# Cross-attention block: block 29 projected in seven products of halves, block 31's query products 1 and 7 in quarters, banks and order written anew

## The chip, the cores and the metric

One core of one Trainium2 chip. The time is that of the device for one launch, in microseconds. PE is TensorE, DVE VectorE, ACT ScalarE, POOL GpSimd; SP issues most transfers.

## The reference

A cross-attention block with adaptive layer norm, in float32. x is 16 x 1024 x 512, the context 16 x 64 x 512, 16 heads of 32.

```python
def _ada_ln(x, c, W_ss, b_ss):
    mu = jnp.mean(x, axis=-1, keepdims=True)
    var = jnp.mean((x - mu) ** 2, axis=-1, keepdims=True)
    h = (x - mu) / jnp.sqrt(var + EPS)
    ss = jax.nn.silu(c) @ W_ss + b_ss
    scale, bias = jnp.split(ss, 2, axis=-1)
    return (1.0 + scale)[:, None, :] * h + bias[:, None, :]
xq = _ada_ln(x_q, t_vec, Wss_q, bss_q)
xkv = _ada_ln(x_kv, t_vec, Wss_kv, bss_kv)
q = (xq @ Wq + bq).reshape(B, Lq, nh, dh)
kv = (xkv @ Wkv + bkv).reshape(B, Lkv, 2, nh, dh)
k, v = kv[:, :, 0], kv[:, :, 1]
scores = jnp.einsum('bqhd,bkhd->bhqk', q, k) / jnp.sqrt(jnp.float32(dh))
attn = jax.nn.softmax(scores, axis=-1)
out = jnp.einsum('bhqk,bkhd->bqhd', attn, v).reshape(B, Lq, H)
return x_q + (out @ Wp + bp)
```

## The kernel before

The queries are worked in 32 blocks of 512 rows (two per batch entry), numbered 0 to 31. The context is worked once, in two groups A and B of eight entries, on the way in.

Large products are not done plainly. A query projection of a block (512 x 512 by 512 x 512) is split into halves and done as seven products of halves instead of eight, by the scheme of Strassen and Winograd: `query_product(i, 1..7)`, each four matmuls of 128x256 (each matmul is two passes on PE, so eight records in the profile). For blocks 4 to 30 the products 1 and 7 are split once more, into seven products of 128x128 each (`quarter_products`, four first and three later, with `quarter_copies` on ACT, three small adds `quarter_adds` on DVE between them, and `feature_quarters` on POOL ahead). The output projection is done in the same manner: `product(i, 1..7)`, with row sums of `ot` on POOL (`row_sum`), sums of weights WT, and results added to the residual r on DVE (`added`, L1116, and L1107 for block 31). Before, block 29 was the one exception: `project`, L974, four plain products, each of four matmuls of 128x512.

The steps of one block, in the order in which its data passes them:

- load x, statistics (`q_stats`, DVE), normalise (`hidden`, ACT), 32x32 transposes to ht (`turn`, DVE), sixteen DMAs to xt (`move`, SP), scale and shift (`scale_features`, ACT), sums of features (`feature_sums`, POOL);
- query products, copied to qt with bias (`query_out`, ACT, L645) or added to it (`query_added`, DVE);
- scores in two halves of the keys, z = 0 and 1 (`score_products`, L738), in two PSUM pairs of banks, `ps`; their maxima per row (`maximum`, DVE, L755) and copies to SBUF (`copied`, ACT);
- `maxima`: both halves' maxima joined and spread to a tile mb (DVE, L784); `subtract`: s minus mb (POOL, L797, one for each half); `weights`: the exponential (ACT, L808);
- `total`: the sum of both halves (POOL, L858); `row_total`: its row sums lt (DVE, L863); `inverse_rows`: the reciprocal (DVE, L878), a DMA to DRAM (ltd) and four back (vr); `spread_rows`: spread to vb (DVE, L891);
- `mix`: weights times values into the pairs po (PE, L936; L947 for blocks 30 and 31); `divided`: po times vb to ot (DVE, L915);
- the output projection, its results added to r, r written out.

Four blocks are in flight. The order on every engine is the order in which these functions are called: on the way in and on the way out a list written out by hand or by a planner, in the middle a `for` loop (i = 3 to 29) that calls each step for the block it is due for. Engines run their instructions in that order and wait for each other by semaphores only. `scores(i)` of a round works beside the query products of block i + 1 and the output products of blocks i - 2 and i - 1.

Of the kernel before, what the change touches and what calls it, by code (L numbers as in the profile page):

```python
# [15 lines left out]
P = 128  # L16
# [4 lines left out]
def cross_attention_block(  # L21
# [182 lines left out]
    BW = 32  # L204
# [526 lines left out]
    def score_products(i, z):  # L731
# [13 lines left out]
        if z == 0:  # L745
            m_tiles[i] = small.tile([P, 2, HPC, NJ], F32, tag="m2", name=f"m2_{i}")
# [51 lines left out]

    l_tiles = {}
# [14 lines left out]

    def again(i, g):
# [7 lines left out]
    def sums(i, z):  # L823
        if z == 0:
            l_tiles[i] = small.tile([P, 2, HPC, NJ], F32, tag="l2", name=f"l2_{i}", bufs=1)
# [35 lines left out]
    def row_total(i):  # L861
        lt_tiles[i] = small.tile([P, HPC, NJ], F32, tag="lt", name=f"lt_{i}", bufs=2)
# [8 lines left out]
    def halves_total(i):  # L871
        lt_tiles[i] = small.tile([P, HPC, NJ], F32, tag="lt", name=f"lt_{i}", bufs=2)
        both(lt_tiles[i].rearrange("p r j -> p (r j)"), l_tiles.pop(i), ALU.add)

    def inverse_rows(i):
# [3 lines left out]
        v = small.tile([P, NC, NJ], F32, tag="vr", name=f"vr_{i}", bufs=2)  # L879
# [4 lines left out]
        vt_rows[i] = v  # L884

# [133 lines left out]
    def biased(i, k):  # L1019

        b = b_first if k == 2 else b_diff
        if i == NB - 1 and k == 2:
            z_halves.append(bank(f"pp_{i}_0", 0))
            z_halves.append(ps_s.tile([P, 2, TB], F32, tag="s", name=f"pp_{i}_0b")[:, 0, :])
# [10 lines left out]
    def output_seed(i):  # L1035

        seeded.add((i, 2))
        acc[3] = bank(f"pp_{i}_2", 3)
        nc.scalar.copy(acc[3], acc[2])
# [24 lines left out]
    def product(i, n):  # L1064
# [12 lines left out]
        if n == 2 and (i, 2) not in seeded:  # L1077
            acc[k] = bank(f"pp_{i}_{n}", k)
        for t in range(2):
            for c in range(HC):  # L1080
# [12 lines left out]
                )  # L1093

# [29 lines left out]
    w_k_sums = big.tile([P, 4, HC, HO], F32, tag="big2", name="w_k_sums")  # L1124
    warm = bank("warm", 1)
    for _ in range(WARM):
        nc.tensor.transpose(warm[:, :P], ident, ident)
    load_x("A")
    load_scale_shift("kv", w_ss_kv, 0)
    q_stats("A", (0,))  # L1130
    q_stats("A", (1,))
    q_stats("A", (2,))
    load_scale_shift("kv", w_ss_kv, 1)
    q_stats("A", (3,))
    q_scale("A")
    load_context_weights(1, 0)
    hidden("A", (0,))
    biases()
    load_context_weights(0, 1)
    scale_shift_rows("kv", 0)  # L1140
    scale_shift_taken("kv", 0)
    turned_features("A", 0)
    hidden("A", (2,))
    hidden("A", (1,))
    turned_features("A", 1)
    hidden("A", (3,))
    scale_shift("kv", 2 * NC, 0)
    turned_features("A", 2)
    turned_features("A", 3)
    modulated("A", 0, 1, nc.vector)  # L1150
    load_context_weights(0, 0)
    modulated("A", 0, 0, nc.scalar)
    scale_shift_rows("kv", 1)
    scale_shift_taken("kv", 1)
    load_x(0)
    modulated("A", 0, 0, nc.vector)
    modulated("A", 0, 1, nc.scalar)
    load_scale_shift("q", w_ss_q, 0)
    column_sums("k", w_k_sb, w_k_sums, (0,))
    scale_shift("kv", 2 * NC, 1)  # L1160
    load_scale_shift("q", w_ss_q, 1)
    column_sums("k", w_k_sb, w_k_sums, (1,))
    modulated("A", 1, 0, nc.scalar)
    column_sums("k", w_k_sb, w_k_sums, (2,))
    modulated("A", 1, 0, nc.vector)
    context_product("A", "v", 1)
    context_product("A", "k", 2)
    modulated("A", 1, 1, nc.vector)
    load_x("B")
    modulated("A", 1, 1, nc.scalar)  # L1170
    feature_sums("A", nc.vector, (0,))
# [697 lines left out]
```

## Time and profile before

| | |
|---|---|
| three runs | 996.85, 997.28, 998.1 us; median 997.28 |
| span of the profiled execution | 996.9 us (the page gives no other time of it) |
| PE busy | 984.2 us |
| DVE, POOL busy | 895.6, 895.4 us |
| ACT busy | 779.3 us |
| granted TensorE clock | 1.000 mean |

Rows of a timeline read: start in us from the span's start, length, engine, line, operation, output<-inputs, shape, count; in brackets the idle time of that engine ahead of the row and what ended it. Matmuls are pipelined, so of PE the distance from one start to the next counts, not the length. In the chain of waits a row is start, length and what ran.

### The profile page before, as it was taken

What the parts mean: (1) busy time and instruction counts of PE and PEld (TensorE: products, weight loads), DVE (VectorE), ACT (ScalarE), POOL (GpSimd) and SP (SyncE); (2) the same over time, 40 slices, a digit from 0 to 9 for tenths busy, and PEclk for the clock granted to TensorE, in tenths of its full rate; (3) what the DMA queues carried; (4) which work ended last, traced back from release to release, by engine and by line L of the source; (5) the groups of instructions that cost most, each with busy time, mean ns of one, the idle gap of its engine ahead of it and who ended that gap; (6) DMA issues with size and microseconds to landing.
All of it is one profiled execution on the core that took longest, in us unless ns stands there. A gap on an engine that the chain in (4) does not pass through costs nothing.

```text
span 996.9 us, 20564 instructions
## 1 busy us (share of the span) xinstructions
PE 984.2 (99%) x7465; PEld 760.7 (76%) x7465; DVE 895.6 (90%) x1318; ACT 779.3 (78%) x1165; POOL 895.4 (90%) x690
## 2 busy tenths in 40 slices
PE   7999999999999999999999999999999999999998
PEld 6878777787777877877778778777787787777756
DVE  7696899999999999999999999999999999987786
ACT  3878878888888888888888888888888888876620
POOL 2677899999999999999999999999999999999681
PEclk9999999999999999999999999999999999999999
DMA  9765655555655555566655555665555555544422
GB/s 308 264 165 151 156 164 156 140 165 180 190 181 176 159 165 152 151 182 186 183 176 152 173 145 155 185 188 178 176 150 175 151 154 182 148 132 130 145 85 97
DMA packets 115188, 165.77 MB, mean 166 GB/s; under 512 B 34920, under 2 KB 46464, under 8 KB 113168
## 3 DMA queue, kind: packets, MB, share of 16 engines
q1 hardware_dynamic: 114704, 163.93, 55.2%
q8 instruction: 59, 0.97, 0.4%
q0 software_dynamic: 384, 0.54, 0.2%
q14 instruction: 41, 0.34, 0.1%
HBM read 79.47 MB, written 34.60 MB: 114 GB/s over the span
## 4 chain that ended last, share of the span: by engine, by line
PE 88%; DMA 4%; DVE 3%; SPq 2%; POOL 1%; issue 1%; ACT 0%; DVEq 0%; POOLq 0%
PE pp L1086 36%; PE pq L534 27%; PE pq L605 10%; PE ps L738 6%; PE po L936 5%; PE pk_A L534 1%; PE pk_B L534 1%; DMA w_k_sb<-in_L_xcond_Wkv_dram 1%; DMA r<-in_x_dram 1%; PE pv_B L534 1%; DMA ltd<-lt 1%; DMA V_B<-stage_B 1%; DMA vr<-ltd 0%; POOL sum L858 0%; DVE l L826 0%
## 5 line engine op out<-in xcount | busy, mean ns | idle before, releaser
L797 POOL TENSOR_TENSOR s<-s,mb 128x2048 f32<-128x2048 f32 x64 | 290.6, 4564 | 20.3 <-DVE mb L784 13.4
L1086 PE MATMUL pp<-w_p_sb,ot 128*128 128x256 f32 x740 | 174.8, 379 | 1.1 <-DVE ot L915 1.1
L764 ACT COPY s<-ps 128x1024 f32<-128x1024 f32 x128 | 129.3, 1013 | 46.1 <-PE ps L738 34.0
L755 DVE TRANSPOSE_TENSOR_REDUCE m<-ps 128x32 f32<-128x1024 f32 x128 | 152.4, 1228 | 10.4 <-PE ps L738 9.3
L1086 PEld LDWEIGHTS pp<-w_p_sb,ot 128*128 128x128 f32 x740 | 138.2, 190 | 20.5 <-issue 2.8
L645 ACT ACTIVATE qt<-pq,bias_t 128x256 f32<-128x256 f32 x256 | 107.8, 475 | 48.8 <-PE pq L605 27.7
L858 POOL TENSOR_TENSOR sum<-s,p 128x2048 f32<-128x2048 f32 x30 | 136.5, 4549 | 1.6 <-ACT p L808 1.6
L1116 DVE TENSOR_TENSOR r<-pp,r 128x512 f32<-128x512 f32 x183 | 120.3, 669 | 13.8 <-ACT xt L442 6.8
L534 PE MATMUL pq<-xt,w_q_sums 128*128 128x256 f32 x512 | 123.8, 385 | 0.0
L534 PEld LDWEIGHTS pq<-xt,w_q_sums 128*128 128x128 f32 x512 | 95.0, 190 | 34.6 <-issue 22.6
L1086 PE MATMUL pp<-WT,ot 128*128 128x256 f32 x492 | 118.4, 383 | 0.0
L1086 PE MATMUL pp<-WT,s 128*128 128x256 f32 x488 | 116.1, 380 | 1.3 <-DVE r L1107 0.8
L817 ACT ACTIVATE s<-s 32x2048 f32<-32x2048 f32 x60 | 114.6, 1910 | 1.8 <-DMA p<-s 0.4
L1086 PEld LDWEIGHTS pp<-WT,ot 128*128 128x128 f32 x492 | 90.9, 190 | 19.1 <-issue 4.2
L1086 PEld LDWEIGHTS pp<-WT,s 128*128 128x128 f32 x488 | 88.2, 190 | 13.1 <-POOL s L1056 1.3
L327 ACT ACTIVATE x<-x,rstdq 128x512 f32<-128x512 f32 x128 | 94.8, 807 | 1.0 <-POOL rstdq L304 1.0
L442 ACT ACTIVATE xt<-xt,ss_q 128x512 f32<-128x512 f32 x124 | 94.0, 809 | 1.0 <-DMA xt<-ht 0.7
L915 DVE TENSOR_TENSOR ot<-po,vb 128x1024 f32<-128x1024 f32 x62 | 73.0, 1219 | 17.6 <-PE po L936 17.4
L286 DVE BATCH_NORM_STATS2 bs<-x 128x6 f32<-128x512 f32 x128 | 85.3, 666 | 0.0
L493 POOL TENSOR_TENSOR xt_sums<-xt 128x512 f32<-128x512 f32 x64 | 81.2, 1269 | 2.0 <-DMA x<-in_x_dram 1.3
L357 DVE STREAM_TRANSPOSE ht<-x 128x512 f32<-128x512 f32 x124 | 77.7, 679 | 4.7 <-DMA xt<-ht 2.2
L891 DVE STREAM_TRANSPOSE vb<-vr 128x2048 f32<-128x2048 f32 (+1 forms) x33 | 73.7, 2236 | 4.4 <-DMA vr<-ltd 4.4
(224 smaller groups left out, 1963.8 us busy)
## 6 DMA issues: line engine op xcount, KB each, us to landing
x<-in_x_dram SPq DMA_DIRECT2D x32, 1024.0 KB, 5.3
r<-in_x_dram SPq DMA_DIRECT2D x32, 1024.0 KB, 5.9
xt<-ht SPq DMA_DIRECT2D x488, 64.0 KB, 2.0
out_dram<-r SPq DMA_DIRECT2D x60, 512.0 KB, 4.7
p<-s SPq DMA_DIRECT2D x60, 256.0 KB, 3.8
wss_kv<-in_L_xcond_Wss_kv_dram SPq DMA_DIRECT2D x4, 512.0 KB, 7.2
wss_q<-in_L_xcond_Wss_q_dram SPq DMA_DIRECT2D x4, 512.0 KB, 11.0
vr<-ltd SPq DMA_DIRECT2D x128, 8.0 KB, 1.7
```

Source lines behind the costliest of these rows:

```text
L327: nc.scalar.activation(dst, src, AF.Identity, bias=rstd[:, 1, j : j + 1], scale=rstd[:, 0, j : j + 1])
L442: nc.scalar.activation(xt[:, :, c, :], xt[:, :, c, :], AF.Identity, scale=ss["q"][:, c, b : b + 1], bias=ss["q"][:, NC + c, b : b + 1],)
L534: nc.tensor.matmul(out_, lhsT=lhsT, rhs=rhs, start=new and m == 0 and c == 0, stop=c == HC - 1, skip_group_check=True,)
L605: nc.tensor.matmul(qa["q", k][:, q * P : (q + 1) * P], lhsT=lhsT, rhs=rhs, start=first and q == 0, stop=True, skip_group_check=True,)
L645: nc.scalar.activation(dst, src, AF.Identity, bias=bq_t[:, o : o + 1])
L755: nc.vector.tensor_reduce(m_tiles[i][:, z, 2 * e : 2 * e + 2, :], s_banks[i, z][e].rearrange("p r (j a) -> p r j a", a=32), AX.X, ALU.max, ...
L764: nc.scalar.copy(s_tiles[i, z][:, 2 * e : 2 * e + 2, :], s_banks[i, z][e])
L797: eng.tensor_tensor(s_tiles[i, z], s_tiles[i, z], mb_tiles[i], ALU.subtract)
L817: nc.scalar.activation(s_tiles[i, 0][at + 32 : at + 64], raw_tiles[i][at : at + 32], AF.Exp, scale=SCALE)
L858: nc.gpsimd.tensor_tensor(t, s_tiles[i, 0], s_tiles[i, 1], ALU.add)
L1086: nc.tensor.matmul(to, lhsT=rows[:, c, t * P : (t + 1) * P], rhs=cols[:, c, :], start=n == 2 and (i, 2) not in seeded and t == 0 and c == ...
L1116: nc.vector.tensor_add(r, a, r)
```

## The change

Four things.

Block 29 is projected by `product(29, 1..7)` like its neighbours, with the bias seeded in PSUM (`biased`, `output_seed`) instead of added to r on POOL; `load_projection(again=True)`, which restored a part of w_p that the weight sums overwrite, is not called any more. Block 30's product 1 is no longer added by itself but seeds the bank of its product 2, as in the blocks before.

Block 31's query products 1 and 7 are done in quarters, 14 matmuls of 128x128 instead of 8 of 128x256.

For block 30, `subtract` of half 1 is done by DVE straight from PSUM (`lowered`), and its copy on ACT goes. Banks and buffers are laid anew (`acc_bank`; lt and vr with one buffer instead of two). A number of new functions is defined and not called (`inner_...`, `exchanged`, `reciprocal_rows` and others); two small constant tiles of theirs are made.

The order is new everywhere. The `for` loop now runs over i = 5 to 27 and is cut at another place: a round begins with the query products of block i and ends with its scores; the blocks before and after are written out. On the way in, the two halves of w_k are loaded in the other order, and product 1 of group A's keys runs ahead of product 2.

```diff
-    load_context_weights(0, 1)
...
-    load_context_weights(0, 0)
+    load_context_weights(0, 0)
+    load_context_weights(0, 1)
...
-        if n == 2 and i >= NB - 2:
-            return 1 if i == NB - 2 else 3
-        return (2 if n in (1, 6, 5, 3) else 3) - (2 if i == NB - 1 else 0)
+        if i == NB - 1 and n == 2:
+            return 4
+        return (2 if n in (1, 6, 5, 3) else 3) - (2 if i in (NB - 3, NB - 1) else 0)
...
+    def lowered(i, e):
+        rs = slice(2 * e, 2 * e + 2)
+        nc.vector.tensor_tensor(
+            s_tiles[i, 1][:, rs, :], s_banks[i, 1][e], mb_tiles[i][:, rs, :], ALU.subtract
+        )
...
-        lt_tiles[i] = small.tile([P, HPC, NJ], F32, tag="lt", name=f"lt_{i}", bufs=2)
+        lt_tiles[i] = small.tile([P, HPC, NJ], F32, tag="lt", name=f"lt_{i}", bufs=1)
...
-    for i in range(3, NB - 2):
+    for i in range(5, NB - 4):
...
+            row_total(a)
...
+        added(b, 7)
+        score_products(i, 0)
+        maximum(i, 0, 0)
...
-    project(y - 1, 0)
+    product(y - 1, 1)
```

In the steady blocks, DVE, from the row sums lt of block 20 to the joined maxima of block 21. A name is tile, block, part, and a running number: `r_19<-pp_19_3` is the add of a product of block 19's output projection (bank 3 holds products 7, and 4), `ps_21_0_1` the second pair of the scores of block 21's half 0. Before:

```order
L863 TENSOR_REDUCE lt_20_6399<-sum_20_6342 128x64
L878 RECIPROCAL lt_20_6399<-lt_20_6399 128x64
L755 TENSOR_REDUCE m2_21_6440<-ps_21_0_0_6422 128x32
L755 TENSOR_REDUCE m2_21_6440<-ps_21_0_1_6423 128x32
L622 TENSOR_TENSOR t_quarters_129<-pq_22_1_6443,t_quarters_129 128x128
L623 TENSOR_TENSOR pq_22_1_6443<-pq_22_1_6443,t_quarters_129 128x256
L624 TENSOR_TENSOR pq_22_1_6443<-pq_22_1_6443,t_quarters_129 128x128
L1116 TENSOR_TENSOR r_19_6143<-pp_19_2_6317,r_19_6143 128x2x256
L755 TENSOR_REDUCE m2_21_6440<-ps_21_1_1_6457 128x32
L755 TENSOR_REDUCE m2_21_6440<-ps_21_1_0_6456 128x32
L775 TENSOR_REDUCE m_21_6496<-m2_21_6440 128x64
L784 STREAM_TRANSPOSE mb_21_6498<-m_21_6496 128x2048
```

And now (L907 is the old L863, L1288 the old L1116, L922 the old L878):

```order
L907 TENSOR_REDUCE lt_20_6380<-sum_20_6335 128x64
L1288 TENSOR_TENSOR r_19_6071<-pp_19_3_6367,r_19_6071 128x2x256
L772 TENSOR_REDUCE m2_21_6419<-ps_21_0_0_6401 128x32
L772 TENSOR_REDUCE m2_21_6419<-ps_21_0_1_6402 128x32
L639 TENSOR_TENSOR t_quarters_129<-pq_22_1_6423,t_quarters_129 128x128
L640 TENSOR_TENSOR pq_22_1_6423<-pq_22_1_6423,t_quarters_129 128x256
L641 TENSOR_TENSOR pq_22_1_6423<-pq_22_1_6423,t_quarters_129 128x128
L1288 TENSOR_TENSOR r_19_6071<-pp_19_2_6312,r_19_6071 128x2x256
L922 RECIPROCAL lt_20_6380<-lt_20_6380 128x64
L772 TENSOR_REDUCE m2_21_6419<-ps_21_1_1_6446 128x32
L772 TENSOR_REDUCE m2_21_6419<-ps_21_1_0_6445 128x32
L792 TENSOR_REDUCE m_21_6499<-m2_21_6419 128x64
```

The add of product 7 (bank 3), which came after mb, stands behind lt, and the reciprocal has moved from there to behind the other add.

On the way out, PE around the first scores of block 31 (`pq_31` are its query products, `pp_28` the output products of block 28, `po_29` the mix of block 29). Before:

```order
L534 MATMUL pq_31_7_8846<-xt_sums_517,w_q_sb_101 128x256 x4
L534 MATMUL pq_31_1_8799<-xt_31_8501,w_q_sums_401 128x256 x4
L1086 MATMUL pp_28_2_8706<-WT_1338,s1_28_8703 128x256 x4
L738 MATMUL ps_31_0_0_8884<-qt_31_8843,K_B_131 32x512 x2
L738 MATMUL ps_31_0_1_8885<-qt_31_8843,K_B_131 32x512 x2
```

And now:

```order
L1002 MATMUL po_29_1_8909<-p_29_8723,V_B_133 32x512
L551 MATMUL pq_31_7_8857<-xt_sums_529,w_q_sb_101 128x256 x4
L551 MATMUL pq_31_1_8764<-xt_31_8532,w_q_sums_404 128x256 x4
L755 MATMUL ps_31_0_0_8943<-qt_31_8851,K_B_131 32x512 x2
L755 MATMUL ps_31_0_1_8944<-qt_31_8851,K_B_131 32x512 x2
```

The output product that stood between the last query product and the scores is gone from there.

Later on PE, the end of block 29's projection and block 30's. Before (128x512 are block 29's plain products):

```order
L974 MATMUL pp_29_2_9051<-w_p_sb_104,ot_29_8949 128x512 x4
L974 MATMUL pp_29_3_9061<-w_p_sb_104,ot_29_8949 128x512 x4
L1086 MATMUL pp_30_2_8990<-w_p_sb_104,ot_30_9048 128x256 x4
L1086 MATMUL pp_30_2_9086<-w_p_sb_104,ot_30_9048 128x256 x4
L1086 MATMUL pp_30_2_8990<-WT_1338,s2_30_9091 128x256 x4
```

And now:

```order
L1155 MATMUL pp_29_1_9062<-WT_1379,ot_29_8926 128x256 x4
L1155 MATMUL pp_29_0_8941<-WT_1379,s1_29_9006 128x256 x4
L1155 MATMUL pp_30_2_9012<-w_p_sb_104,ot_30_9076 128x256 x4
L1155 MATMUL pp_29_1_9062<-w_p_sb_104,ot_29_8926 128x256 x4
L1155 MATMUL pp_29_0_8941<-WT_1379,ot_29_8926 128x256 x4
```

Block 30's first product now stands among the seven of block 29.

More of the change, by code (lines that the diff above doesn't have):

```diff
@@ L1076, in product @@
         k = acc_bank(i, n)
-        if n == 2 and (i, 2) not in seeded:
+        if n == 2 and (i, 2) not in seeded and k < 4:
             acc[k] = bank(f"pp_{i}_{n}", k)
@@ new lines, in cross_attention_block @@
+    hidden(6, (3,))
+    maximum(3, 1, 1)
+    added(1, 6)
+    feature_quarters(4, 7)
+    maximum(3, 1, 0)
+    query_product(4, 6)
+    copied(3, 1, 1)
+    feature_sums(4, nc.gpsimd, (3,))
+    added(1, 7)
+    hidden(6, (1,))
+    maxima(3)
+    product(1, 5)
+    added(1, 5)
+    copied(3, 1, 0)
+    spread_rows(2)
+    product(1, 4)
+    q_stats(7, (0,))
+    product(1, 3)
+    hidden(6, (0,))
+    query_out(4, 2)
+    quarter_products(4, 7, True)
+    quarter_copies(4, 7)
+    added(1, 3)
@@ new lines, in cross_attention_block @@
+    again(26, 1)
+    query_product(28, 6)
+    product(25, 4)
+    spread_rows(26)
+    copied(27, 1, 1)
+    subtract(27, zs=(0,))
+    q_stats(31, (0,))
+    query_out(28, 2)
+    copied(27, 1, 0)
+    quarter_products(28, 7, True)
+    added(25, 4)
+    query_out(28, 6)
+    product(25, 3)
+    quarter_copies(28, 7)
+    mix(26)
+    quarter_adds(28, 7)
+    q_stats(31, (1,))
+    weights(27, 0)
+    quarter_products(28, 7, False)
+    turn(30, (0,))
+    scale_features(29, (2,))
+    query_out(28, 7)
@@ new lines, in cross_attention_block @@
+    copied(28, 0, 0)
+    feature_sums(29, nc.gpsimd, (2,))
+    score_products(28, 1)
+    row_sum(26, 3)
+    q_scale(31)
+    added(26, 2)
+    row_total(27)
+    inverse_rows(27)
+    biased(26, 3)
+    move(30, ks=(3,))
+    product(26, 7)
+    added(26, 6)
+    query_seed(29)
+    maximum(28, 1, 1)
+    feature_quarters(29, 7)
+    maximum(28, 1, 0)
+    again(27, 0)
+    maxima(28)
+    added(26, 7)
+    query_product(29, 2)
+    again(27, 1)
+    subtract(28, zs=(0,))
+    query_product(29, 6)
@@ new lines, in cross_attention_block @@
+    weights(28, 0)
+    added(26, 3)
+    mix(27)
+    query_product(29, 5)
+    divided(27, (0,))
+    query_out(29, 7)
+    query_added(29, 5)
+    query_product(29, 4)
+    query_product(29, 3)
+    divided(27, (1,))
+    row_sum(27, 0)
+    scale_features(30, (2,))
+    biased(27, 2)
+    load_residual(27)
+    product(27, 1)
+    row_sum(27, 2)
+    added(26, 4)
+    hidden(31, (3,))
+    weights(28, 1)
+    feature_quarters(30, 1)
+    query_out(29, 3)
+    query_added(29, 4)
+    quarter_products(30, 1, True)
@@ new lines, in cross_attention_block @@
+    again(28, 0)
+    query_product(30, 6)
+    product(27, 7)
+    query_out(30, 6)
+    feature_sums(30, nc.gpsimd, (3,))
+    quarter_adds(30, 7)
+    query_product(30, 5)
+    added(27, 7)
+    added(27, 5)
+    product(27, 4)
+    subtract(29, zs=(0,))
+    again(28, 1)
+    copied(29, 1, 1)
+    copied(29, 1, 0)
+    subtract(29, zs=(1,))
+    quarter_products(30, 7, False)
+    added(27, 4)
+    product(27, 3)
+    query_out(30, 7)
+    scale_features(31, (0,))
+    added(27, 3)
+    mix(28)
@@ L1772, in cross_attention_block @@
-    mix(y)
-    spread_rows(y)
-    divided(y)
-    project(y - 1, 2, later=True)
-    weights(z, 0)
-    projected(y - 1, 2)
+    maximum(z, 0, 1)
+    score_products(z, 1)
+    output_seed(y - 1)
+    inverse_rows(y)
+    product(y - 1, 2)
+    row_sum(y - 1, 0)
+    copied(z, 1, 0)
+    row_sum(y - 1, 2)
+    maximum(z, 1, 0)
+    biased(y, 2)
+    product(y - 1, 6)
+    copied(z, 1, 1)
+    row_sum(y - 1, 1)
+    maximum(z, 1, 1)
+    maxima(z)
+    added(y - 1, 2)
+    added(y - 2, 4)
+    mix(y)
```

1573 lines of the change are left out of this document (1010 added, 563 removed).

## The prediction

> **What bounds the kernel now.** I read the page first (busy shares, slices), then who waited for whom on TensorE, then one steady stretch of the timeline on each engine, then the way out.
>
> ```profile
> span 996.9 us, 20564 instructions
> ...
> PE 984.2 (99%) x7465; PEld 760.7 (76%) x7465; DVE 895.6 (90%) x1318; ACT 779.3 (78%) x1165; POOL 895.4 (90%) x690
> ```
>
> TensorE (PE) is busy 984.2 of 996.9 us, so all its idle time is 12.7 us. The waits on it show where:
>
> ```profile
> PE pc L210 <- DMA early<-in_cond_dram: 2.6, 1, 2.6
> PE pk_A L534 <- DMA w_k_sb<-in_L_xcond_Wkv_dram: 1.4, 1, 1.4
> PE ps_kv L248 <- DMA wss_kv<-in_L_xcond_Wss_kv_dram: 1.3, 2, 1.0
> PE pp L1086 <- DVE ot L915: 1.1, 1, 1.1
> ```
>
> The first three are the way in, the last the way out. Between them there is nothing to win:
>
> ```profile
> 110.00:860.00 750.00, 749.76 (x5745) 582.18 (x5744) 706.78 (x1018) 628.50 (x915) 724.97 (x552) 1.00 0.57 168
> ```
>
> From 110 to 860 us PE is busy 749.76 of 750 at a granted clock of 1.00; POOL with 724.97 is the next. One block takes what lies between two equal places of the chain of waits:
>
> ```profile
> 477.04 3.46 PE pp L1086 x16
> ...
> 505.56 3.46 PE pp L1086 x16
> ```
>
> 505.56 - 477.04 = 28.52 us. The other engines have little to spare, though, and one stretch shows how little. Blocks early in the run were still catching up, so there nothing waited for PE, and POOL and DVE ran their own loop freely. POOL:
>
> ```profile
> 190.53 9.09 POOL L797 TENSOR_TENSOR s<-s,mb 128x2048 f32<-128x2048 f32 x2
> ...
> 202.19 4.55 POOL L858 TENSOR_TENSOR sum<-s,p 128x2048 f32<-128x2048 f32 x1
> ...
> 218.79 9.09 POOL L797 TENSOR_TENSOR s<-s,mb 128x2048 f32<-128x2048 f32 x2
> ```
>
> and DVE, which takes over when sum ends (202.19 + 4.55 = 206.74) and hands back with mb (216.34 + 2.31 = 218.65):
>
> ```profile
> 206.78 2.31 DVE L863 TRANSPOSE_TENSOR_REDUCE lt<-sum 128x64 f32<-128x2048 f32 x1 [0.39 <-POOL sum L858]
> 209.12 0.55 DVE L878 RECIPROCAL lt<-lt 128x64 f32<-128x64 f32 x1
> 209.68 2.38 DVE L755 TRANSPOSE_TENSOR_REDUCE m<-ps 128x32 f32<-128x1024 f32 x2
> ...
> 212.94 0.68 DVE L1116 TENSOR_TENSOR r<-pp,r 128x512 f32<-128x512 f32 x1
> 213.60 2.38 DVE L755 TRANSPOSE_TENSOR_REDUCE m<-ps 128x32 f32<-128x1024 f32 x2
> 216.01 0.29 DVE L775 TENSOR_REDUCE m<-m 128x64 f32<-128x128 f32 x1
> 216.34 2.31 DVE L784 STREAM_TRANSPOSE mb<-m 128x2048 f32<-128x2048 f32 x1
> 218.58 0.65 DVE L1116 TENSOR_TENSOR r<-pp,r 128x512 f32<-128x512 f32 x1
> 219.15 0.67 DVE L286 BATCH_NORM_STATS2 bs<-x 128x6 f32<-128x512 f32 x1
> ```
>
> This is a closed loop: subtract, sum, lt, reciprocal, maxima of scores half 0, quarter adds, r, maxima of half 1, mb, next subtract. Free-running it takes 218.79 - 190.53 = 28.26 us. Later it waits a little for PE in each round:
>
> ```profile
> 466.37 2.38 DVE L755 TRANSPOSE_TENSOR_REDUCE m<-ps 128x32 f32<-128x1024 f32 x2 [0.26 <-issue]
> ```
>
> 28.26 + 0.26 = 28.52. So PE sets the pace with 0.26 us to spare per block; whatever enters that loop beyond 0.26 us is paid in every block.
>
> **The change, part by part.**
>
> *Block 29's projection.* Four products of 128x512 become seven of halves. Spacing of the rows, since starts are what PE pays:
>
> ```profile
> 947.68 7.11 PE L974 MATMUL pp<-w_p_sb,ot 128*128 128x512 f32 x16 [0.33 <-PE ps L738]
> 954.72 2.35 PE L947 MATMUL po<-s,V_B 32*32 32x512 f32 x64
> 957.00 7.13 PE L974 MATMUL pp<-w_p_sb,ot 128*128 128x512 f32 x16
> 963.97 3.62 PE L1086 MATMUL pp<-w_p_sb,ot 128*128 128x256 f32 x16
> ```
>
> and, for products of halves, from the steady part:
>
> ```profile
> 458.01 1.89 PE L534 MATMUL pq<-xt_sums,w_q_sb 128*128 128x256 f32 x8
> 459.73 1.89 PE L1086 MATMUL pp<-w_p_sb,ot 128*128 128x256 f32 x8
> ```
>
> Removed: 7.04 + 6.97 = 14.0. Added: 7 x 1.72 = 12.1. Net -1.9 us, all on PE's path. Beside it POOL gets four row sums for four bias adds, DVE five adds of halves for four, ACT a few copies of bias and seed at 78% busy: nothing, as long as PE's products cover them; if the cover is gone it shows in the way out (below). The second load of part of w_p goes; nothing waited for it. One subtract of block 30 (half of the 9.09) moves from POOL to DVE, which reads the scores from PSUM, and two ACT copies go: nothing, since it leaves the fuller engine. The buffers of lt and vr go from two to one; their readers are a block older than the next writer: nothing.
>
> *Block 31's query products 1 and 7.* Eight passes of 128x256 become fourteen of 128x128 for each:
>
> ```profile
> 447.46 0.38 PE L605 MATMUL pq<-xt_sums,w_q_sums 128*128 128x128 f32 x2
> 447.69 0.83 PE L605 MATMUL pq<-t_quarters,w_p_sb 128*128 128x128 f32 x6
> 448.36 1.89 PE L1086 MATMUL pp<-w_p_sb,ot 128*128 128x256 f32 x8
> ```
>
> Eight passes take 448.36 - 447.46 = 0.90, fourteen 1.58, against 1.72: -0.14 each at best, zero if the switch between shapes eats it. I take -0.2 for the two. The Trainium skill ("TensorE: Matmul & The Clock Gate", Back-to-back issue gap) states about 81 ns per matmul sustained at N = 128; by it the fourteen would take 1.13 us, the two products would save 1.2 instead of 0.2, and the time below would be 1001.8. The trace has 0.90 / 8 = 112 ns, and it decides.
>
> *Way in.* The half of w_k that product 1 and 2 of group A read is now loaded ahead of the other half, and product 1 runs ahead of 2.
>
> ```profile
> 16.80 1.27 POOL L467 TENSOR_TENSOR w_k_sums<-w_k_sb 128x512 f32<-128x512 f32 x1 [13.07 <-DMA w_k_sb<-in_L_xcond_Wkv_dram]
> ```
>
> ```profile
> 19.24 3.69 PE L534 MATMUL pk_A<-xk_A,w_k_sb 128*128 128x256 f32 x16 [1.42 <-DMA w_k_sb<-in_L_xcond_Wkv_dram]
> ```
>
> The first half is there at 16.80, so the wait of 1.42 goes. What is late next is POOL's w_k_sums, which now start at 19.2 in place of 16.8; three of 1.27 end near 23, when PE has used up four products (15.8 + 4 x 1.72 = 22.7), and behind them the scale-and-shift weights, whose loads are not brought forward. I take -1.0, between -1.9 (POOL's and PE's wait both gone) and +0.5 (all handed to the next load).
>
> *The steady blocks.* This is where the price lies. On PE only the order of mix and the last three 128x128 products changes, and products 3 and 4 swap; both stay back to back. SP now issues eight of a block's sixteen writes of xt ahead of the reciprocal's round trip (ltd, vr) and eight behind it, where it was twelve and four: vb's rows come earlier relative to their use, the features later, within what ACT idles (78% busy). But on DVE the r add of product 7 (L1116) now stands between lt and the maxima of half 0, where the reciprocal stood, and the reciprocal between the other r and the maxima of half 1. Both places lie inside the loop; before, product 7's add came after mb (the row at 218.58), outside. So the loop gains exactly one r add: 213.60 - 212.94 = 0.66 when a maximum follows, 219.15 - 218.58 = 0.57 when something else follows; I take 0.60. Loop: 28.26 + 0.60 = 28.86, over PE's 28.52 by 0.34. That DVE cannot let the maxima pass the add is what the lt row shows: it sat 0.39 us waiting for POOL with other work queued. The loop is closed 23 times (the for loop's i = 5 to 27, from mb of block 4 to mb of block 27): 23 x 0.34 = 7.8 us, less some 0.2 that PE can be behind before it has to wait: +7.6. Ends: 23 x 0.31 - 0.2 = +6.9 (add at 0.57) and 23 x 0.40 = +9.2 (0.66). After block 27 the maxima of half 0 come ahead of lt, the loop is open, and PE sets the pace again.
>
> *Way out.* Gone: the 1.1 for ot and the 0.33 ahead of the four products. New, by the order: the scores of block 31 stand directly behind its query product 3, with nothing between to cover the copy of the result:
>
> ```profile
> 937.72 1.89 PE L1086 MATMUL pp<-WT,s 128*128 128x256 f32 x8
> ```
>
> ```profile
> 937.92 0.84 ACT L645 ACTIVATE qt<-pq,bias_t 128x256 f32<-128x256 f32 x2 [0.45 <-PE pq L534]
> ```
>
> The query product before that row ended where it starts (937.72), its copy at 938.76: +1.0. The second half of the scores follows one product (1.72) later, while DVE has a lt (2.31) and two maxima (2.38) to do first, the lt partly earlier: 0 to 2, I take +0.8. Block 30's first product needs ot, and DVE has three r adds (2.0), vb (2.3, as long as mb) and ot between block 31's mb and that: 0 to 2, +1.3. Together 3.1 new and 1.4 gone; since PE waiting at one of the three places shortens the next wait, I take +1.0 net, between -1.4 and +3.
>
> Sum on the profiled span: 996.9 - 1.9 - 0.2 - 1.0 + 7.6 + 1.0 = 1002.4. The page gives no time of this execution but the span; the median of the three runs (997.28) is 0.4 above it, so 1002.8 us.
>
> **The rivals.**
> *The loop stays open (faster).* The add of product 7 would have to cost under 0.26 us inside the loop, or sum to end earlier than by the old rows. For it: all other orders of the block are near the old ones. Against: an r add is never under 0.57 from start to start, and the free round of 28.26 has no gap longer than 0.1 in it. It decides at 0.26 us. Time: 1002.8 - 7.6 = 995.2.
> *PE loses more elsewhere.* Between mb and the adds that release product 7's last three products DVE now has one r, three pairs of row statistics and vb; if vb's rows or x come late there, PE waits too. At 0.2 us a block: 1002.8 + 23 x 0.2 = 1007.4.
> *The change gives back what it saves.* The loop holds the pace (as in the first rival) and the way out costs its upper end: 995.2 + 2 = 997.2, the same time.
>
> **How the numbers follow.** Forecast (loop closed, 999.5 to 1005.5): 0.72. Loop open: 0.14. Same: 0.07. More lost: 0.07. A measurement of this kernel tells 0.2% (2.0 us) from no change. Faster by that is below 995.3: half of the open loop and some of the ways to be better on the way in and out, 0.12. Within: the other half, the third rival, the forecast's lowest edge, 0.13. Slower: 0.75. The range of 995.0 to 1006.0 leaves out about 2 in 10: half of the open loop, the upper rival, and the tails. The forecast's own range is 999.5 to 1005.5.
>
> **What would show it.** Right: blocks spaced 28.8 to 28.9 us between 230 and 800 us; DVE's r of product 7 directly between lt and the maxima with no idle before the maxima; POOL idle before subtract 0.5 to 0.7; PE with a wait of about 0.3 per block, on DVE's maxima (the scores' banks) or quarter adds; spacing back to 28.5 after block 27; PE's busy time down by about 2. Wrong: PE gapless through the steady blocks at 28.5, which would leave only ways in and out; or a block spacing above 29, with a wait that I have not named.

## The result, and the profile after

The changed kernel takes 1048.38 us (median of 4, 1046.6 to 1050.3) against 997.24 us (996.85 to 998.1): ratio 1.0509, 95% interval 1.0493 to 1.0524. It is slower, as forecast, but by 51 us, not by 5.5, and far outside the range. The profiled execution took 1050.3 us with a span of 1048.5.

The page, the lines that answer to those of before:

```profile
span 1048.5 us, 20722 instructions
...
PE 1018.8 (97%) x7501; PEld 770.4 (73%) x7501; DVE 898.7 (86%) x1326; ACT 779.0 (74%) x1169; POOL 895.7 (85%) x695
```

TensorE is "busy" 34.6 us longer, although by the forecast's count of passes (1.9 + 0.2) it has 2.1 us less to do. The windows of the steady part, busy time and number of records of each engine, after and then before:

```profile
260.00:860.00 600.00, 598.80 (x4494) 448.00 (x4494) 547.10 (x790) 484.03 (x711) 559.79 (x432) 1.00 0.57 164
```

```profile
260.00:860.00 600.00, 600.00 (x4627) 466.03 (x4626) 567.79 (x823) 505.45 (x737) 579.02 (x442) 1.00 0.57 169
```

Both look full, but the same 600 us hold 4494 matmul records in place of 4627, 3% fewer, at the same clock of 1.00. So the time is lost inside rows that count as busy. I put scores next to scores (start of the first half of a block's scores in the timeline of TensorE):

| | before | after | lag |
|---|---|---|---|
| block 0 | 60.68 | 61.91 | +1.2 |
| block 3 | 151.24 | 166.41 | +15.2 |
| block 5 | 208.38 | 231.15 | +22.8 |
| block 27 | 835.84 | 882.61 | +46.8 |
| end of span | 996.9 | 1048.5 | +51.6 |

Three places, then: +22.8 on the way in, +24.0 in the 22 steady rounds (28.52 us before, 29.57 in nearly all rounds after), +4.8 on the way out.

**Steady.** TensorE, first and second half of one block's scores, after, and the second half of one block before:

```profile
497.90 1.14 PE L755 MATMUL ps<-qt,K_A 32*32 32x512 f32 x32
498.97 0.49 PE L622 MATMUL pq<-xt,w_q_sb 128*128 128x128 f32 x2
...
501.79 2.08 PE L755 MATMUL ps<-qt,K_A 32*32 32x512 f32 x32
503.81 0.71 PE L622 MATMUL pq<-xt,w_q_sb 128*128 128x128 f32 x4
```

```profile
468.96 1.14 PE L738 MATMUL ps<-qt,K_A 32*32 32x512 f32 x32
470.03 0.71 PE L605 MATMUL pq<-xt,w_q_sb 128*128 128x128 f32 x4
```

The second half takes 503.81 - 501.79 = 2.02 us to the next start, the first 1.07; before, the second half took 470.03 - 468.96 = 1.07 too. The 0.95 between them is a wait in the middle of a group. The list of TensorE's matmul waits doesn't have it; it shows in that of its weight loads, which I had passed over because they overlap the matmuls (time in all, times, longest; after, then before):

```profile
PEld ps L755 <- ACT s L781: 21.4, 26, 1.1
```

```profile
PEld ps L738 <- ACT s L764: 10.0, 30, 0.4
```

The list points at the place and the releaser but not at the size: it grows by 11.4 us, where the starts of the rounds show 24.0.

ScalarE and VectorE at the same place:

```profile
500.48 1.01 ACT L781 COPY s<-ps 128x1024 f32<-128x1024 f32 x1 [2.40 <-DVE m L772]
501.39 0.38 ACT L633 COPY t_quarters<-pq 128x256 f32<-128x256 f32 x1
501.65 1.03 ACT L781 COPY s<-ps 128x1024 f32<-128x1024 f32 x1
```

```profile
496.42 2.29 DVE L907 TRANSPOSE_TENSOR_REDUCE lt<-sum 128x64 f32<-128x2048 f32 x1
498.63 0.65 DVE L1288 TENSOR_TENSOR r<-pp,r 128x512 f32<-128x512 f32 x1
499.21 2.37 DVE L772 TRANSPOSE_TENSOR_REDUCE m<-ps 128x32 f32<-128x1024 f32 x2
```

And ScalarE before (its scores start at 465.07):

```profile
466.45 1.01 ACT L764 COPY s<-ps 128x1024 f32<-128x1024 f32 x1 [1.18 <-PE ps L738]
467.36 0.38 ACT L616 COPY t_quarters<-pq 128x256 f32<-128x256 f32 x1
467.65 1.01 ACT L764 COPY s<-ps 128x1024 f32<-128x1024 f32 x1
```

A pair of score banks has two readers, the maximum on VectorE and the copy on ScalarE. In these rows they do not read one pair at the same time: the one called later waits for the other. Before, ScalarE copied pair 1 while VectorE took the maxima of pair 0, and its first copy began 1.38 us after the scores. Now it copies pair 0 first and so waits for VectorE (2.40, "<-DVE m"); that copy begins 2.58 us after the scores, the quarter copy stands behind it, and pair 1 is free only at 502.68. TensorE has nothing to do in its order but to stop inside the next scores. The Trainium skill ("PSUM — Partial Sum Buffer", PSUM bank collisions raise a hardware error) says that ScalarE and VectorE reading the same 32 partitions of one bank at once raise an error, and that the hardware neither arbitrates nor stalls. The rows above agree in so far as the two reads are in turn; no run here shows what a collision does.

VectorE, meanwhile, has the add of product 7 exactly where the forecast put it, and the maxima start 1.31 us after the scores, where they started 1.30 after before (466.37 - 465.07).

**Way in.** TensorE's two long waits, and VectorE's ahead of them:

```profile
PE pv_B L551 <- DVE stage_B L703: 6.3, 1, 6.3
PE pv_B L551 <- ACT K_B L683: 3.7, 1, 3.7
```

```profile
78.10 1.25 DVE L772 TRANSPOSE_TENSOR_REDUCE m<-ps 128x32 f32<-128x1024 f32 x1 [5.78 <-ACT s L781]
113.02 1.25 DVE L772 TRANSPOSE_TENSOR_REDUCE m<-ps 128x32 f32<-128x1024 f32 x1 [6.98 <-ACT s L781]
```

The same rule the other way round: here the maximum is called after the copy and waits for ScalarE, whose queue is late. Behind the first of these maxima come mb, subtract and the exponentials, and behind those on ScalarE K_B's copy; behind the second comes mb, and then stage_B on VectorE. K_B's copy and stage_B free banks for TensorE. Each wait costs more than itself; TensorE's windows with the granted clock as third number from the end, and the matmuls that follow the waits:

```profile
94.00:96.00 2.00, 2.00 (x5) 1.64 (x6) 1.38 (x3) 2.00 (x5) 2.00 (x1) 0.50 0.00 0
119.00:121.00 2.00, 1.69 (x4) 1.43 (x5) 1.97 (x5) 0.00 (x0) 2.00 (x1) 0.50 0.00 0
```

```profile
93.91 3.78 PE L551 MATMUL pv_B<-w_v_sb,xk_B 128*128 128x256 f32 x8 [3.70 <-ACT K_B L683]
119.31 3.78 PE L551 MATMUL pv_B<-w_v_sb,xk_sums_B 128*128 128x256 f32 x8 [6.28 <-DVE stage_B L703]
```

That is 3.78 us for eight passes that take 1.89 elsewhere.

**Way out.** Block 31's scores:

```profile
998.39 1.05 PE L755 MATMUL ps<-qt,K_B 32*32 32x512 f32 x4 [0.53 <-ACT s L781]
1000.59 2.01 PE L755 MATMUL ps<-qt,K_B 32*32 32x512 f32 x28 [1.15 <-DVE m L772]
...
1010.51 1.97 PE L1155 MATMUL pp<-WT,ot 128*128 128x256 f32 x8 [1.41 <-ACT pp L1099]
```

### The profile page after: what moved, and what is told of

The parts are those of the page before. It is cut to its first block, busy times and chain, and to the rows that moved or that the text cites. A ratio compares the mean times of both kernels' runs of the same rounds, so it can differ in the third digit from the quotient of the medians.

```text
span 1048.5 us, 20722 instructions
## 1 busy us (share of the span) xinstructions
PE 1018.8 (97%) x7501; PEld 770.4 (73%) x7501; DVE 898.7 (86%) x1326; ACT 779.0 (74%) x1169; POOL 895.7 (85%) x695
## 4 chain that ended last, share of the span: by engine, by line
PE 78%; DVE 6%; DMA 5%; ACT 3%; POOL 3%; SPq 2%; issue 1%; DVEq 0%; ACTq 0%; POOLq 0%
PE pp L1155 32%; PE pq L551 23%; PE pq L622 8%; PE ps L755 8%; PE po L1002 4%; DMA x<-in_x_dram 2%; POOL s L814 2%; DVE m L772 1%; SPq L399 1%; PE pk_A L551 1%; ACT s L781 1%; POOL sum L902 1%; PE pv_A L551 1%; DMA p<-s 1%; DMA ltd<-lt 1%
## 5 line engine op out<-in xcount | busy, mean ns | idle before, releaser
L814 POOL TENSOR_TENSOR s<-s,mb 128x2048 f32<-128x2048 f32 x63 | 286.7, 4557 | 49.3 <-DVE mb L801 23.4
L1155 PE MATMUL pp<-w_p_sb,ot 128*128 128x256 f32 x756 | 179.7, 381 | 0.5 <-DVE ot L981 0.3
L781 ACT COPY s<-ps 128x1024 f32<-128x1024 f32 x126 | 125.1, 1017 | 71.4 <-DVE m L772 60.3
L1288 DVE TENSOR_TENSOR r<-pp,r 128x512 f32<-128x512 f32 x188 | 126.0, 672 | 41.6 <-ACT xt L459 28.8
L1155 PEld LDWEIGHTS pp<-w_p_sb,ot 128*128 128x128 f32 x756 | 143.5, 191 | 24.6 <-issue 2.8
L1155 PE MATMUL pp<-WT,ot 128*128 128x256 f32 x508 | 122.2, 384 | 2.8 <-ACT pp L1099 1.6
L1155 PE MATMUL pp<-WT,s 128*128 128x256 f32 x504 | 119.9, 381 | 0.0
L344 ACT ACTIVATE x<-x,rstdq 128x512 f32<-128x512 f32 x128 | 103.4, 817 | 5.7 <-POOL rstdq L305 5.6
L551 PEld LDWEIGHTS pq<-xt,w_q_sums 128*128 128x128 f32 x512 | 95.0, 190 | 15.2 <-ACT qt L662 1.7
L374 DVE STREAM_TRANSPOSE ht<-x 128x512 f32<-128x512 f32 x124 | 82.4, 687 | 10.1 <-ACT x L344 6.6
L981 DVE TENSOR_TENSOR ot<-po,vb 128x1024 f32<-128x1024 f32 x64 | 77.4, 1215 | 3.0 <-PE po L1002 2.6
```

The source lines that it names most:

```text
L344: nc.scalar.activation(dst, src, AF.Identity, bias=rstd[:, 1, j : j + 1], scale=rstd[:, 0, j : j + 1])
L551: nc.tensor.matmul(out_, lhsT=lhsT, rhs=rhs, start=new and m == 0 and c == 0, stop=c == HC - 1, skip_group_check=True,)
L781: nc.scalar.copy(s_tiles[i, z][:, 2 * e : 2 * e + 2, :], s_banks[i, z][e])
L814: eng.tensor_tensor(s_tiles[i, z], s_tiles[i, z], mb_tiles[i], ALU.subtract)
L1155: nc.tensor.matmul(to, lhsT=rows[:, c, t * P : (t + 1) * P], rhs=cols[:, c, :], start=n == 2 and (i, 2) not in seeded and t == 0 and c == ...
L1288: nc.vector.tensor_add(r, a, r)
```

## The experiments

"In turn" below means that ScalarE copies the pair that VectorE is not reading. Each run had runs of the kernel before beside it on its chip (997.7 to 998.1 us).

**First: the copies exchanged in the changed kernel's steady loop.**

```diff
-        copied(i, 0, 0)
+        copied(i, 0, 1)
...
-        copied(i, 0, 1)
+        copied(i, 0, 0)
```

> The changed kernel, in whose steady loop ScalarE copies half (i,0,1) of the scores first and (i,0,0) after the quarter copy; nothing else moves. Theory A (ScalarE and VectorE read one score bank only in turn, so a copy that follows the maximum of the same half waits for it, and with it the quarter copy, the quarter adds and the bank that the next scores need): the stall of 0.94 inside the second half of the scores goes, the quarter adds no longer wait 0.29, and the block interval is that of the loop over GpSimd, 16.25 + 0.04 + 12.66 - 0.29 + 0.14 = 28.8 us instead of 29.57. 23 rounds x 0.77 = 17.7 less: 1030.7 us. Rival (the forecast's loop alone, the order of copies is hidden): interval 29.57 as before, 1048.4 us, or at most 23 x 0.29 = 6.7 less, 1041.7 us.

1034.21 us (ratio 1.0362, 1.0346 to 1.0379): 14.2 less. The stall is gone and ScalarE no longer waits for VectorE:

```profile
523.94 1.14 PE L755 MATMUL ps<-qt,K_A 32*32 32x512 f32 x32
525.01 0.71 PE L622 MATMUL pq<-xt,w_q_sb 128*128 128x128 f32 x4
```

```profile
521.41 1.01 ACT L781 COPY s<-ps 128x1024 f32<-128x1024 f32 x1 [1.18 <-PE ps L755]
```

The usual round is 28.62 now, 0.95 less than 29.57. But single rounds take 29 to 30.4, so the mean is 29.11, against 29.61 in the changed kernel. Of the 14.7 us by which the span is shorter, 10.9 lie in the 22 rounds and 1.7 behind them; 2.1 are already there at block 5's scores, ahead of the edit, and belong to this execution's way in. From 260 to 860 us TensorE waits ten times for quarter adds, 5.0 us in all; the rest of the longer rounds is not traced.

**Second and third: the add of product 7 back behind mb, without and with the exchanged copies.**

```diff
             maxima(a)
+        if i > 5:
+            added(i - 3, 7)
...
-        added(b, 7)
```

> The changed kernel with the add of product 7 put back behind the maxima and mb, as the kernel before has it; the copies stay as the change has them. The forecast's loop: the whole excess over TensorE's 28.52 hangs on this add, so the interval is 28.52 and the time 1048.4 - 23 x 1.05 = 1024 us. Theory A (a second loop over TensorE: product 2, its add, ht, qt, lt, maxima, the copies in turn, second half of the scores): only the 0.58 of the add leaves it, interval 29.57 - 0.58 = 28.99, time 1048.4 - 23 x 0.58 = 1035 us, and the stall inside the second half of the scores is still there, some 0.4 us.

> The changed kernel with both edits: the copies the other way round and the add of product 7 behind mb. Theory A: nothing of either loop is over TensorE's work, interval 28.52, time 1048.4 - 23 x 1.05 = 1024 us. Rival (something else in the changed loop, such as the wait of product 2's add, keeps its own pace): interval 28.8 or more, 1031 us or more.

1050.14 us (1.0504 to 1.0539) and 1039.08 us (1.0399 to 1.0431). Both theories fell: taking out the add that I had called the price gains nothing (rounds of 29.67), and with the copies exchanged it costs 4.9 (usual rounds of 29.08 against 28.62, but in the mean, single longer ones included, 29.22 against 29.11). In the second run the maxima wait for the scores 0.5 us a block, which is all that leaving out the add buys. So the changed loop was not closed over VectorE and GpSimd at all; TensorE's own stall set the pace. In the third the add stands among what VectorE does between mb and product 7's quarter adds. The last of these begins 17.36 us after block 12's scores in the third run and 16.90 in the first, and TensorE's products behind it 17.81 and 17.34. The list of waits has only part of that:

```profile
PE pq L622 <- DVE pq L641: 2.7, 8, 0.6
PE pq L622 <- ACT s L836: 2.2, 12, 0.2
```

**Fourth: the maxima of the way in ahead of the copies.**

```diff
     maximum(0, 1, 1)
+    maximum(0, 1, 0)
...
-    maximum(0, 1, 0)
...
     score_products(1, 1)
+    maximum(1, 1, 1)
+    maximum(1, 1, 0)
```

(and the two calls of block 1 taken out where they were)

> The changed kernel, steady loop untouched; on the way in the maxima of the second score half of blocks 0 and 1 are written directly behind their scores, ahead of the copies of the same halves. Theory A (VectorE waits 5.78 and 6.98 us there for ScalarE's copy of the same bank, and mb, the subtracts, K_B's copy and stage_B are late by that): TensorE's waits of 3.7 and 6.3 us before the value products of group B go, and with them the stretches at a granted clock of 0.50 behind them, some 5 us more: about 1048.4 - 15 = 1033 us. Rival (the copies are late with everything else, because GpSimd or the loads of x are late on the new way in): the waits stay within 2 us of what they are, 1046 to 1049 us.

1037.58 us (1.0385 to 1.0416): 10.8 less, where theory A had 15. Both long waits are gone and so are the stretches at half clock:

```profile
94.00:96.00 2.00, 2.00 (x11) 1.75 (x10) 2.00 (x1) 0.49 (x1) 1.92 (x2) 1.00 0.87 193
```

Block 5's scores start at 219.40 in place of 231.15, still 11.0 behind the kernel before. From block 3's to block 5's scores it takes 64.7 us, as the changed kernel does, against 57.1 before; that is 7.6 of the 11.

**Fifth: add and reciprocal in the places of the change, in the kernel before.**

```diff
+        added(b, 7)
         score_products(i, 0)
...
         added(b, 6)
+        if i > 3:
+            inverse_rows(a)
...
-        added(b, 7)
...
-        inverse_rows(i)
...
+    inverse_rows(NB - 3)
```

> The kernel before, in whose steady loop two VectorE instructions take the places that the change gives them: the add of product 7 stands between lt and the maxima of half 0, the reciprocal behind product 6's add. Nothing else moves. The forecast's price (0.60 us more in the loop of subtract, sum, lt, maxima and mb, 28.86 against TensorE's 28.52): interval 28.86 in 27 rounds, 997.3 + 9.2 = 1006.5 us. Rival, by the rows of the first experiment (there lt to the end of mb took 12.07 us with both inside, against 11.87 before, so the two trade places for 0.20 us, less than the 0.26 to spare): interval 28.52, 997.3 us.

1148.69 us (1.1478 to 1.1532), a miss of both. `inverse_rows` also issues the reciprocal's round trip, and now sixteen writes of xt stood ahead of it in SyncE's queue:

```profile
522.58 11.00 SPq L382 DMA_DIRECT2D xt<-ht  x16
...
534.30 0.47 SPq L881 DMA_DIRECT2D ltd<-lt  x1
```

```profile
542.64 2.31 DVE L891 STREAM_TRANSPOSE vb<-vr 128x2048 f32<-128x2048 f32 x1 [4.62 <-DMA vr<-ltd]
```

The run says nothing on the add; it prices a place in a queue, some 5.6 us a block. TensorE waits 4.0 of it for ot, which needs vb (84.7 us in 21 rounds); the granted clock is 0.958 in the mean.

**Sixth: the changed order of copies, alone, in the kernel before.**

```diff
-        copied(i, 0, 1)
+        copied(i, 0, 0)
...
-        copied(i, 0, 0)
+        copied(i, 0, 1)
```

> The kernel before, in whose steady loop ScalarE copies (i,0,0) first and (i,0,1) after the quarter copy, as the change has it. Nothing else moves. Theory B (the copy of a half waits for the maximum of the same half, the second copy stands behind it and the quarter copy, and TensorE waits 0.94 us inside the second half of the scores in each block, whatever VectorE does): interval 28.52 + 1.0 = 29.5 us, 27 rounds, about 997.3 + 27 = 1024 us. Rival (the order of copies is hidden in this order of products, or VectorE's loop takes up the wait): 28.5 to 28.6, 997 to 1000 us.

1023.13 us (1.0243 to 1.0273): two exchanged calls cost 25.3 us, as theory B had it. The round goes from 28.52 to 29.47, and the rows are those of the changed kernel:

```profile
506.60 2.10 PE L738 MATMUL ps<-qt,K_A 32*32 32x512 f32 x32
508.63 0.71 PE L605 MATMUL pq<-xt,w_q_sb 128*128 128x128 f32 x4
```

```profile
505.30 1.01 ACT L764 COPY s<-ps 128x1024 f32<-128x1024 f32 x1 [2.40 <-DVE m L755]
```

With the first run, this shows the cause of the steady blocks from both sides.

**Seventh and eighth: the three stretches apart.** All functions are the changed kernel's. The list of calls is that of before up to one call, `score_products(27, 0)` in the seventh and `score_products(5, 0)` in the eighth, and behind it come the calls that are left, in the changed order.

> The order of the kernel before until the scores of block 27, and from there the changed kernel's order, with block 29 in seven products and block 31's query products 1 and 7 in quarters. By the two traces (scores of block 27 to the end: 161.06 before, 165.89 after): 997.3 + 4.8 = 1002 us. By the forecast's terms (-1.9 - 0.2 + 1.0): 996.2 us.

> The order of the kernel before until the scores of block 5, and from there the changed kernel's order. If the three stretches add up (way in +22.8, steady blocks +24, way out +4.8): 1048.4 - 22.8 = 1025.6 us with an interval of 29.57. Rival (the steady interval of 29.57 is a state that the late way in sets up, and the engines ahead keep it away): interval 28.6 to 28.9 and 1003 to 1011 us.

1000.95 us (1.0022 to 1.0051) and 1025.88 us (1.0271 to 1.0302). By these times the way out costs +3.1, the steady part 1025.88 - 1000.95 = +24.9, the way in 1048.38 - 1025.88 = +22.5. Such differences always add up to the whole; what tells is that two of them agree with the stretches of the trace (+24.0 and +22.8; the way out had +4.8 there). The usual steady round takes 29.57 in the eighth run too, with the better way in. In the seventh it is 28.52, with the banks, the single buffers of lt and vr and all other functions of the changed kernel: what the steady rounds lose is the order alone. TensorE's waits on the way out, in the seventh run:

```profile
PE pp L1155 <- ACT pp L1099: 1.7, 1, 1.7
PE ps L755 <- DVE m L772: 1.2, 1, 1.2
PE ps L755 <- ACT qt L662: 0.6, 1, 0.6
PE ps L755 <- ACT s L781: 0.5, 1, 0.5
```

**Ninth and tenth: the forecast's main term again.** The add of product 7 alone ahead of the maxima; then the fifth run with the last eight writes of xt moved behind the reciprocal's round trip.

```diff
+        added(b, 7)
         score_products(i, 0)
...
-        added(b, 7)
```

```diff
+            inverse_rows(a)
+            if i + 2 < NB:
+                move(i + 2, ks=(2,))
+                move(i + 2, ks=(3,))
```

> The kernel before, in whose steady loop the add of product 7 stands between the reciprocal and the maxima of half 0; the reciprocal stays behind lt. The forecast's arithmetic (start to start 0.60 us in a loop of 28.26 against TensorE's 28.52): interval 28.86, 27 rounds x 0.34 = 9.2, 1006.7 us. Rival (VectorE reaches these maxima ahead of the scores by more than the trace's 0.26, and what it loses there it makes up before lt): interval 28.52, 997.5 us.

> As the fifth run (the add of product 7 in the reciprocal's place, the reciprocal behind product 6's add), and the last eight writes of xt of a block now stand behind the reciprocal's write and reads in SyncE's queue, as the change has them. Theory (the fifth run lost its time to the reciprocal's round trip behind sixteen writes of xt, and the add itself costs nothing): vb no longer waits 4.6 us, interval 28.52 to 28.6, 997 to 1000 us. The forecast's price: 28.86, 1006.7 us. If the round trip is still late: over 1010 us.

The ninth: 1002.41 us (1.0032 to 1.0062), +4.5, between the two. The usual round is 28.62. VectorE and GpSimd are now the closed loop of the forecast:

```profile
492.90 2.31 DVE L863 TRANSPOSE_TENSOR_REDUCE lt<-sum 128x64 f32<-128x2048 f32 x1 [0.22 <-POOL sum L858]
...
495.72 0.63 DVE L1116 TENSOR_TENSOR r<-pp,r 128x512 f32<-128x512 f32 x1
496.26 2.37 DVE L755 TRANSPOSE_TENSOR_REDUCE m<-ps 128x32 f32<-128x1024 f32 x2
...
502.84 2.31 DVE L784 STREAM_TRANSPOSE mb<-m 128x2048 f32<-128x2048 f32 x1
```

From lt to the end of mb it is 502.84 + 2.31 - 492.90 = 12.25 us, 0.38 more than the 11.87 before, not 0.60. The add itself takes 0.54 from its start to the maxima's; the rest of the chain is 0.16 shorter than in the early stretch of the forecast, and no run shows why. So the loop is real, and 0.10 over TensorE in place of 0.34. The tenth took 1069.71 us (1.0699 to 1.0766). That is in the range of its third theory, but not for the reason given there: vb waits only 14.6 us in 19 rounds for the round trip, and now ScalarE waits for the writes of xt that were moved.

```profile
ACT xt L442 <- DMA xt<-ht: 62.4, 20, 4.2
```

**Eleventh: the way out in turn.** The seventh run, block 31's copies exchanged, the add of block 29's product 2 ahead of the last maxima.

```diff
-    copied(31, 0, 0)
     copied(31, 0, 1)
+    copied(31, 0, 0)
...
-    copied(31, 1, 0)
+    copied(31, 1, 1)
...
+    added(29, 2)
     maxima(31)
```

> The seventh run (order of before to block 27, the changed way out behind it) with three moves at block 31: of each score half ScalarE copies the bank that VectorE is not reading (copies of a half exchanged, twice), and the add of block 29's product 2 stands ahead of block 31's last maxima. Theory (TensorE's waits of 0.53 + 1.15 for the scores' banks and 1.70 for a bias copy behind that add come from the order alone): 3 us less, 998 us. Rival (they turn into waits for the next thing, as mb is then later): 1000 to 1001 us.

998.08 us, ratio 1.0002 (0.9993 to 1.0012): 2.9 less than the seventh, and the kernel before's time.

**Twelfth: more in the first run's loop.** Product 7's quarter copy ahead of the copies of half 1, the exchanged rows ahead of four writes of xt.

```diff
             quarter_copies(i, 7)
+            copied(a, 1, 0)
+            copied(a, 1, 1)
...
+            swapped(a)
             move(f, ks=(0,))
```

> The first run (changed kernel, copies of half 0 exchanged) with two more moves in the steady loop: ScalarE copies product 7's quarters ahead of the two copies of score half 1, and SyncE writes the exchanged rows of a block ahead of four writes of xt. Theory (what is left over 28.52 in that run is product 7's quarter adds, late behind ScalarE's queue, every block by 0.1 and in some blocks by 1 us when ScalarE waits for the exchanged rows): interval 28.52 to 28.6 in all blocks, 1034.2 - 22 x 0.55 = 1022 us. Rival (VectorE's order, three row statistics and vb ahead of those adds, is what is late): 29.0 as in the first run, 1032 to 1034 us.

1044.93 us (1.0449 to 1.0492), 10.7 worse than the first run, and outside both theories. The usual round is 29.10. The mix writes into the same pairs of banks as the scores, so it waits for the copies that I had pushed back (weight loads of TensorE):

```profile
PEld po L1002 <- ACT s L781: 16.3, 40, 0.8
```

**Thirteenth and sixteenth: the way out further.** The eleventh run with block 27's copies in turn (the sixteenth), and with products 1 and 2 of block 29 ahead of block 31's two score halves as well (the thirteenth).

```diff
-    copied(27, 0, 0)
+    copied(27, 0, 1)
...
+    product(29, 1)
+    output_seed(29)
     score_products(31, 0)
...
+    product(29, 2)
     score_products(31, 1)
```

> The eleventh run with three more moves: the copies of block 27's half 0 exchanged (a stall of 1.1 us in its scores), block 29's product 1 and its seed ahead of block 31's first scores, product 2 ahead of the second (waits of 0.56 and 0.53 there). Theory (the way out's waits are all order): 998.1 - 1.1 - 0.9 = 996.1 us, 1.7 us under the kernel before, near the 2.1 us by which the passes are fewer. Rival (VectorE's maxima of block 31, now later, pass the wait on to the next product): 997 to 998 us.

> The eleventh run with the copies of block 27's half 0 exchanged, nothing else. Theory (the stall of 1.1 us in that block's scores is the order of copies, as in the steady blocks, and nothing behind it takes it up): 998.1 - 1.1 = 997.0 us, 0.1% under the kernel before, a tie by this measurement. Rival (the blocks behind it wait for VectorE or GpSimd, which then come first): 998 us.

The thirteenth took 1000.32 us (1.0012 to 1.0030), over both of its theories, the sixteenth 997.5 us (ratio 1.0000, 0.9990 to 1.0009). In the thirteenth the 0.56 us wait became one of 1.6 for product 1's bias copy and another of 1.6 for ot:

```profile
PE pp L1155 <- ACT pp L1099: 1.6, 1, 1.6
PE pp L1155 <- DVE ot L981: 1.6, 1, 1.6
```

The sixteenth is the best order found with block 29 in seven products: a tie with the kernel before.

**Fourteenth: in turn everywhere.** The edits of the first, fourth and eleventh run in the changed kernel.

> The changed kernel with the edits of the first, fourth and eleventh run together: in the steady loop and at block 31 ScalarE copies the bank that VectorE is not reading, on the way in the maxima of half 1 of blocks 0 and 1 stand directly behind their scores. If they add up: 1048.4 - 14.2 - 10.8 - 2.9 = 1020.5 us. Rival (where one wait goes another place sets the pace): over 1024 us.

1017.57 us (1.0178 to 1.0209). They add up, and a little more: 30.8 of the 51 us go with these moves, nearly all of which concern the order of two readers (the eleventh run's edit, 2.9 us, also moves an add). Of what is left in the trace, 8.1 us lie ahead of block 5's scores and 10.9 in the steady rounds: 28.62 is the usual one, but the mean is 29.01, with one of 31.4. The longer rounds are not traced. On the way out 0.2 are left.

**Fifteenth: where the rest of the way in is lost.** As the eighth, cut at `score_products(2, 0)`.

> The order of the kernel before until the scores of block 2, the changed kernel's order from there. Theory (the whole loss of the way in lies ahead of block 2's scores): as the eighth run, 1025.9 us. Rival (the changed order of blocks 2 to 4, with rounds of 32 us in the fourth run where the kernel before has 28.5, costs some 7 to 11 us by itself): 1032 to 1037 us.

1040.6 us (1.0410 to 1.0438), more than either theory. The cut made a wait of its own: VectorE stands 11.1 us at the statistics of an x that is loaded late by this mixed order, and TensorE 9.2 at the scores.

```profile
DVE bs L287 <- DMA x<-in_x_dram: 11.1, 1, 11.1
PE ps L755 <- ACT s L781: 10.1, 2, 9.2
```

What can be used is behind it: block 3's to block 5's scores take 64.5 us here, as in the changed kernel (64.7) and the fourth run (64.7). The changed order of blocks 3 and 4 loses 7.4 to 7.6 us whatever comes ahead of it. Which calls in it do that was not tried; nor were the 3.5 us left ahead of block 3 (22.8 - 11.75 - 7.6).

## Why the prediction was wrong

The sign held, and the size did not: +51 in place of +5.5.

- *"On PE only the order of mix and the last three 128x128 products changes ... both stay back to back."* This is the step that failed. I followed the change on PE, DVE, SP and POOL; of ScalarE in the steady blocks the forecast says only that the later features fall "within what ACT idles (78% busy)". The new order of `copied`, which stands in neither its sum nor its rivals, it put at nothing without a reason. The share of ScalarE's busy time was no argument: the price is when its copies can begin. That is 0.95 us in the usual round, shown by the first and sixth run.
- *The loop through the add of product 7, +0.34 a block, +7.6.* The mechanism exists: the ninth run shows it closed, at 28.62. The term was mis-sized, 4.5 us in 27 rounds against 9.2 by the forecast's own 0.34. I took the add at a start-to-start 0.60, but the whole chain from lt to mb grew by 0.38. (The forecast's upper end, "23 x 0.40 = +9.2", lacks the 0.2 that it takes off the other two values; it should be +9.0.) In the changed kernel the add cost nothing, since TensorE at 29.57 was slower than that loop; the second run, without the add, is no faster.
- *The other rival, "PE loses more elsewhere".* Its place (quarter adds of product 7, late behind row statistics and vb) is real but showed only when the copies were in turn (first and third run).
- *Way in, -1.0.* I costed the loads of w_k and nothing behind them. Block 0's scores come no earlier: they start at 61.4 to 62.5 us in the seven traces with the changed way in and at 59.1 to 62.3 in the eleven with the old one, 1.6 later in the mean. Blocks 0 to 4 then lose another 21.6: about 11 by readers in turn and the clock, 7.6 in blocks 3 and 4, the rest not traced.
- *Way out, +1.0, block 29 -1.9, block 31 -0.2.* Their sum was -1.1; the seventh run has +3.1. Of the places named, the scores of block 31 behind product 3 and their second half do wait, 0.56 and 0.53 + 1.15; block 30's first product waits 0.3 for ot in place of 1.3; and 1.7 for a bias copy was not named. The 2.1 us of passes do not come through as time. In the sixteenth run, from block 27's scores to the end and from start to start, the output products take 1.6 us less than before, but the query products 0.4 and the scores 0.8 more, and TensorE's waits are 2.7 us in place of 2.5.
- *"Wrong: ... a block spacing above 29, with a wait that I have not named."* That is what came.

## What to carry to other kernels

Where a bank has two readers, list them in call order for each bank: the later one waits, and everything behind it on its engine waits too. Let the engines read opposite banks and swap; here two exchanged calls are worth 25 us of 998. And do not read "TensorE 100% busy, no waits" as no loss: compare the number of records in equal windows, or the start-to-start of equal groups, and read the waits of the weight loads.

## What the runs showed of the hardware

A long pause of TensorE is paid twice. After waits of 3.70 and 6.28 us the granted clock was 0.50, and eight passes took 3.78 us in place of 1.89; behind a wait of 1.10 us (at 84.30) it stayed at 1.00, and without the long waits it is 1.00 throughout (fourth run, 60 to 130 us). The Trainium skill ("TensorE: Matmul & The Clock Gate", Part 1: The HAM clock gate) gives half rate after an idle window of about 3.4 us, which agrees with these two. In the fifth run a wait of 3.25 us was enough: the clock was 0.50 from 549 to 551 us, behind it.

The Trainium skill also says there that the window runs freely. Block 31's scores may be a case of that, but the runs do not settle it: with the same waits of 0.53 and 1.15 us, together well under 3.4, the 28 matmuls behind them took 2.01 us in the changed kernel (granted clock 0.58 from 1000 to 1002 us) and 1.14 in the seventh run (1.00 from 951 to 953 us):

```profile
951.69 1.14 PE L755 MATMUL ps<-qt,K_B 32*32 32x512 f32 x28 [1.15 <-DVE m L772]
```
